# One of four sums in each feed-forward unit: VectorE's addition from PSUM, or a ScalarE copy and a GpSimd addition

## The chip, the cores and the metric

The kernel runs on one core of a Trainium2 chip. A core has a matrix engine (TensorE, PE in the profile; its weight loads are PEld), three engines that work on tiles (VectorE is DVE, ScalarE is ACT, GpSimd is POOL), an engine that issues transfers (SyncE, SP), and DMA queues. Each engine takes its instructions in a fixed order. Matrix products land in PSUM; all else lies in SBUF.

The metric is the device time of one execution in microseconds (us), as the median of several runs.

## The reference, cut to what matters

Two graph layers run one after the other on 128 graphs of 128 nodes with 256 features each, in fp32. Each layer ends with a feed-forward network over all nodes, with 1024 hidden units:

```python
# layer 0, after two graph-attention steps
h = layernorm(residual + h, g_ln1, b_ln1)
ff = relu(h @ w_ff1 + b_ff1) @ w_ff2 + b_ff2
x = layernorm(h + ff, g_ln2, b_ln2)
# layer 1, after 8-head attention with 4 relations
x = layernorm(src + attn_out, g1, beta1)
ff = gelu(x @ W1 + b1) @ W2 + b2
out = layernorm(x + ff, g2, beta2)
```

The change touches the first product of each of the two networks, `h @ w_ff1` and `x @ W1`.

## The kernel before, in words

**Tiling.** Four graphs make a group (512 nodes), so there are 32 groups. Five stages work on a group: load, graph attention (`gat`), the feed-forward of layer 0 with Relu (`ff0`), the attention of layer 1, and the feed-forward of layer 1 with Gelu (`ff1`). Every stage is a Python generator that yields a planned duration after each step. A loop at the end of the kernel keeps all stages of all groups in a heap by due time and always advances the earliest. So the stages of neighbouring groups are interleaved: while one group is in `ff1`, the next ones are in the attention and in `ff0`. Their steps repeat with a period of some 96 us.

**Order on the engines.** Between fixed planned times (`KEPT`, 280 to 3260 for TensorE) the order in which the loop emits TensorE's instructions is binding, and so is the order of SP's transfers. The other engines are ordered by the framework's scheduler, which works with its own estimates of time; no instruction of theirs is placed ahead of the TensorE instruction emitted before it. Every pool of buffers is shared by all stages. The PSUM pool `mm` has six buffers of one bank each: all products except `av` take one and give it back when the last reader is done.

**The feed-forward.** `feed_forward` (L289) computes the hidden layer with seven products in place of eight. The input and the weights are cut into halves in both directions; sums of the blocks are formed once (`weight_sums` for the weights, `moving_sums`, L283 to L286, on GpSimd for the moving side), and the seven block products are combined by additions. The hidden features are made in two units of two blocks each, `unit(0)` and `unit(2)`; I call them the first and the second unit. A unit has three PSUM tiles of 128x512, `chain`, `side` and `p`, and two SBUF tiles of twice that size, `lo` and `hi`, both named `fT`. The last index in `lo[:, :, 0]` picks one half of the nodes. A unit has four steps:

1. Products 1 into `chain` and 5 into `side`. ScalarE copies `chain` to half 0 of `lo` (L313) and `side` to half 1 of `hi` (L314).
2. Product 6 is added to `chain`, 2 goes to `p`, 3 is added to `side`. ScalarE copies `chain` to half 1 of `lo` (L320); VectorE adds `p` and `side` to the halves of `lo` (L321, L322).
3. Product 7 is added to `chain` (L307 records all of the products). VectorE adds `chain` to half 1 of `hi` (L325). ScalarE applies Relu or Gelu to `lo` (L327).
4. Product 4 is added to `chain`. ScalarE applies the function to `chain` into half 0 of `hi`, and to half 1 of `hi` in place (L333).

In the loop after `unit` the steps of the two units alternate: first, second, first, second, and so on. Each product is one instruction of 128x256 per block, which the trace shows as two matmuls, so a product of a unit is four matmuls. Between the steps of the units, other stages put their products. After step 4 comes the second product of the network (L350), which takes `lo` and `hi` as its weights.

**Other lines that the prediction names.** L239 scales rows in a layer norm on ScalarE, with factors that GpSimd computes (L233 to L237). L245 is the gain or offset of a norm on GpSimd, in pieces of 128x512 or 128x256. L351 adds the second product to the tokens on VectorE. L373 to L386 are the softmax of the graph attention: L373 and L384 on ScalarE, L380 and L381 on VectorE, L386 on GpSimd. L397 is the first product of the graph attention and L398 its copy by ScalarE; L405, L406 and L415 are its later products and copies. L429 and L435 are the query and key products of the attention, L449 the scores, L455 their maxima on VectorE, L459 the exponential on ScalarE, L461 its scaling on GpSimd, L475 the four masks of a graph (VectorE, 128x1024), L482 and L483 the values and their bias, L494 the weighted sum (`av`), L498 its copy by ScalarE, L532 and L533 the output product and its addition. L262 is a transposition on VectorE ahead of a pair of transfers. L260 is a copy after a transposition on TensorE, which only the first and the last groups use.

Of the kernel before, what the change touches and what calls it, by code (L numbers as in the profile page):

```python
# [57 lines left out]
def graph_layers(ctx: ExitStack, tc: tile.TileContext, a: dict, out: bass.AP):  # L58
# [8 lines left out]
    nc = tc.nc  # L67
# [156 lines left out]
    def normalised(y, first=0, n=G):  # L224

        y = y[:, first:first + n]
        mv = sm.tile([P, n, 2], F32, name="mv")
        for b in range(n):
            st = sm.tile([P, 6], F32, name="st")
            nc.vector.bn_stats(st, y[:, b])  # L230
            nc.vector.bn_aggr(mv[:, b], st)
        rstd = sm.tile([P, n], F32, name="rstd")
        nc.gpsimd.tensor_scalar(rstd, mv[:, :, 1], EPS, None, op0=OP.add)  # L233
        nmr = sm.tile([P, n], F32, name="nmr")
        nc.gpsimd.tensor_scalar(nmr, mv[:, :, 0], -1.0, None, op0=OP.mult)
        nc.gpsimd.tensor_tensor(rstd, rstd, mhalf[:, :n], OP.pow)
        nc.gpsimd.tensor_mul(nmr, nmr, rstd)  # L237
        for b in range(n):
            nc.scalar.activation(y[:, b], y[:, b], AF.Identity, bias=nmr[:, b:b + 1], scale=rstd[:, b:b + 1])  # L239

    def affine(y, k, b, n, engine=nc.gpsimd):


        for op, v in zip((OP.mult, OP.add), ln[k]):
            engine.tensor_tensor(y[:, b:b + n], y[:, b:b + n], v[:, None, :].to_broadcast([P, n, D]), op)  # L245
# [26 lines left out]
    def features(y, direct):  # L272

        t = t_tile().rearrange("p (b c n) -> p b c n", b=G, c=DC)
        blocks = t.rearrange("p b c n -> p (b c) n")
        transposed(y.rearrange("p b (c f) -> p (b c) f", f=P), blocks, direct, blocks)
        return t

    def moving_sums(hT):

        b11, b21, b12, b22 = (hT[:, h:h + G // 2, c] for h in (0, G // 2) for c in range(DC))
        t1, t2, t4 = (wk.tile([P, G // 2, N], F32, name=f"t{i}") for i in (1, 2, 4))
        nc.gpsimd.tensor_sub(t1, b12, b11)  # L283
        nc.gpsimd.tensor_sub(t2, b22, t1)
        nc.gpsimd.tensor_sub(b12, b22, b12)
        nc.gpsimd.tensor_sub(t4, t2, b21)  # L286
        return None, b11, b21, b22, t4, t1, t2, b12

    def feed_forward(y, before, direct, win, bin_, wout, func, by=G):  # L289


        hT = features(y, direct)
        yield TIMES["lead ff0" if before == "01" else "lead ff1"]
        hs = moving_sums(hT)
        yield TIMES["sums"]
        fT = [None] * FC

        def unit(f0):

            lo, hi = (wk.tile([P, 2, 2, T // 2], F32, name="fT", bufs=FC // 2) for _ in range(2))  # L300
            for i in range(2):
                fT[f0 + i] = lo[:, i].rearrange("p h t -> p (h t)")
                fT[FC // 2 + f0 + i] = hi[:, i].rearrange("p h t -> p (h t)")

            def product(p, k, first=False):
                for i in range(2):
                    nc.tensor.matmul(p[:, i], win[k][:, ts(f0 + i, P)], hs[k], start=first and i == 0, stop=True,  # L307
                                     skip_group_check=True)

            chain, side = (ps.tile([P, 2, T // 2], F32, name="mm") for _ in range(2))  # L310
            product(chain, 1, True)
            product(side, 5, True)
            nc.scalar.copy(lo[:, :, 0], chain)  # L313
            nc.scalar.copy(hi[:, :, 1], side)  # L314
            yield
            p = ps.tile([P, 2, T // 2], F32, name="mm")
            product(chain, 6)
            product(p, 2, True)
            product(side, 3)
            nc.scalar.copy(lo[:, :, 1], chain)  # L320
            nc.vector.tensor_add(lo[:, :, 0], lo[:, :, 0], p)  # L321
            nc.vector.tensor_add(lo[:, :, 1], lo[:, :, 1], side)  # L322
            yield
            product(chain, 7)
            nc.vector.tensor_add(hi[:, :, 1], hi[:, :, 1], chain)  # L325
            for i in range(2):
                nc.scalar.activation(lo[:, i], lo[:, i], func, bias=bin_[:, f0 + i:f0 + i + 1])  # L327
            yield
            product(chain, 4)
            for h, p in enumerate((chain, hi[:, :, 1])):  # L330
                for i in range(2):
                    f = FC // 2 + f0 + i
                    nc.scalar.activation(hi[:, i, h], p[:, i], func, bias=bin_[:, f:f + 1])  # L333
            yield

        units = [unit(0), unit(2)]
        for n, now in enumerate(((0,), (1,), (0,), (1,), (0,), (1,), (0,), (1,))):
            for u in now:
                next(units[u])
            if n in (2, 4):  # L340
                affine(y, before, n - 2, 2)
            yield TIMES["ff unit"]
        yield TIMES["ff2"]

        late = sorted(range(FC), key=lambda f: f % (FC // 2) // 2)
        for b2_ in range(0, G, 2):
            p = ps.tile([P, 2, D], F32, name="mm")
            for b in (b2_, b2_ + 1):
                for n, f in enumerate(late):
                    nc.tensor.matmul(p[:, b - b2_], fT[f][:, ts(b, N)], wout[:, f], start=n == 0, stop=n == FC - 1)  # L350
            nc.vector.tensor_add(y[:, b2_:b2_ + 2], y[:, b2_:b2_ + 2], p)  # L351
            yield TIMES["ff half"]
            if (b2_ + 2) % by == 0:
                normalised(y, b2_ + 2 - by, by)
        return y
# [313 lines left out]
```

## Time and profile before

| What | Value |
|---|---|
| median of 3 runs | 3207.63 us (3207.33 to 3208.44) |
| the profiled execution's own time | 3206.17 us |
| its span, first to last instruction | 3204.4 us |
| mean granted TensorE clock | 0.99 |
| busy: ScalarE | 1688.0 us |
| L325, the addition in question | 128 of 128x512, 81.5 us in all, 672 ns each |
| L320, a ScalarE copy of the same shape | 128, 586 ns each |
| L245 on GpSimd, 128x512 and 128x256 | 1276 ns and 739 ns each |

The profile is one execution. A row of a timeline gives the start and the duration in us, the engine, the line, the operation, the tiles (written <- read), the shapes and how many were merged into the row; in brackets follows how long the engine was idle before it and which instruction ended that. A row of waits gives who waited for whom, then the total in us, the number of times, and the longest. A wait for several things is put down to the one that came last by the profile, which can be the wrong one. The ends of matmuls are modelled, so a row of TensorE overlaps the next by some 0.2 us; the start of the next is the better mark.

### The profile page before, as it was taken

What the parts mean: (1) busy time and instruction counts of PE and PEld (TensorE: products, weight loads), DVE (VectorE), ACT (ScalarE), POOL (GpSimd) and SP (SyncE); (2) the same over time, 40 slices, a digit from 0 to 9 for tenths busy, and PEclk for the clock granted to TensorE, in tenths of its full rate; (3) what the DMA queues carried; (4) which work ended last, traced back from release to release, by engine and by line L of the source; (5) the groups of instructions that cost most, each with busy time, mean ns of one, the idle gap of its engine ahead of it and who ended that gap; (6) DMA issues with size and microseconds to landing.
All of it is one profiled execution on the core that took longest, in us unless ns stands there. A gap on an engine that the chain in (4) does not pass through costs nothing. (4 is left out here: it accounts for less than half of the span.)

```text
span 3204.4 us, 55197 instructions
## 1 busy us (share of the span) xinstructions
PE 3123.5 (97%) x20160; PEld 2381.1 (74%) x20160; DVE 2021.8 (63%) x3666; ACT 1688.0 (53%) x5063; POOL 1378.1 (43%) x1738
## 2 busy tenths in 40 slices
PE   7989999999999999999999999999999999999988
PEld 6756777777777777777777777777777777777666
DVE  3666666656566666576666576666576666576563
ACT  4435556555555455555455555455555465555443
POOL 2314345445345344345344345344345344345342
PEclk8999999999999999999999999999999999999999
DMA  4244454444454444454444454444454444453310
GB/s 163 60 106 97 105 116 106 103 101 97 104 118 104 104 99 100 101 121 103 106 99 100 100 122 102 107 98 101 100 122 100 108 94 102 103 122 82 83 34 14
DMA packets 1156399, 320.82 MB, mean 100 GB/s; under 512 B 902944, under 2 KB 1126688, under 8 KB 1156000
## 3 DMA queue, kind: packets, MB, share of 16 engines
q1 hardware_dynamic: 1156128, 317.29, 43.5%
q8 instruction: 160, 2.62, 0.3%
q14 instruction: 111, 0.91, 0.1%
HBM read 187.58 MB, written 129.62 MB: 99 GB/s over the span
## 5 line engine op out<-in xcount | busy, mean ns | idle before, releaser
L475 DVE SCALAR_TENSOR_TENSOR m<-adj,eT 128x1024 f32<-128x1024 f32 x512 | 598.5, 1212 | 240.7 <-DMA eT<-zd 178.2
L245 POOL TENSOR_TENSOR tok<-tok,ln_rows 128x512 f32<-128x512 f32 (+1 forms) x636 | 668.8, 1060 | 42.2 <-PE mm L256 14.8
L461 POOL TENSOR_TENSOR e<-e,s 128x512 f32<-128x512 f32 x256 | 266.4, 1041 | 661.0 <-DVE s L460 629.1
L459 ACT ACTIVATE e<-mm,nm 128x128 f32<-128x128 f32 x1024 | 360.0, 375 | 203.6 <-DVE nm L455 180.5
L482 PE MATMUL mm<-wv,T 128*128 128x512 f32 x1024 | 466.0, 598 | 0.0
L350 PE MATMUL mm<-wf,fT 128*128 128x256 f32 x2048 | 456.9, 381 | 0.0
L350 PE MATMUL mm<-w,fT 128*128 128x256 f32 x2048 | 455.6, 381 | 1.2 <-DVE v L483 1.2
L350 PEld LDWEIGHTS mm<-w,fT 128*128 128x128 f32 x2048 | 387.5, 190 | 74.7 <-issue 23.7
L350 PEld LDWEIGHTS mm<-wf,fT 128*128 128x128 f32 x2048 | 387.4, 190 | 62.3 <-ACT wh L406 7.9
L482 PEld LDWEIGHTS mm<-wv,T 128*128 128x128 f32 x1024 | 192.6, 191 | 200.2 <-issue 191.6
L239 ACT ACTIVATE tok<-tok,nmr,rstd 128x256 f32<-128x256 f32 x512 | 269.3, 594 | 136.4 <-POOL nmr L237 123.8
L351 DVE TENSOR_TENSOR tok<-tok,mm 128x512 f32<-128x512 f32 x128 | 87.8, 686 | 294.9 <-PE mm L350 283.0
L386 POOL TENSOR_TENSOR e<-e,s 128x512 f32<-128x512 f32 (+1 forms) x68 | 67.2, 989 | 470.4 <-DVE s L385 375.2
L494 PE MATMUL av<-m,v 128*32 128x128 f32 x8192 | 254.9, 276 | 6.0 <-DVE m L475 3.5
L494 PEld LDWEIGHTS av<-m,v 128*32 128x32 f32 x8192 | 218.2, 111 | 52.7 <-issue 43.5
L283 POOL TENSOR_TENSOR t<-T 128x256 f32<-128x256 f32 x64 | 46.6, 728 | 485.2 <-DMA T<-zd 485.2
L459 ACT ACTIVATION_READ_ACCUMULATOR e<-mm,nm 128x1 f32 x1024 | 219.4, 214 | 0.0
L455 DVE TENSOR_REDUCE nm<-mm 128x4 f32<-128x512 f32 x256 | 162.8, 676 | 60.3 <-PE mm L449 60.1
L483 DVE TENSOR_TENSOR v<-mm,bv 128x512 f32<-128x512 f32 x256 | 167.4, 683 | 49.3 <-PE mm L482 49.3
L307 PE MATMUL mm<-T,w 128*128 128x256 f32 x768 | 196.9, 386 | 0.2 <-ACT T L260 0.2
L307 PE MATMUL mm<-T,wf 128*128 128x256 f32 x768 | 193.6, 382 | 0.0
L373 ACT ACTIVATE e<-e,wh 128x128 f32<-128x128 f32 x240 | 77.7, 410 | 208.8 <-DMA e<-zsd 208.8
(123 smaller groups left out, 5093.0 us busy)
## 6 DMA issues: line engine op xcount, KB each, us to landing
zd<-e SPq DMA_DIRECT2D x496, 128.0 KB, 3.1
eT<-zd SPq DMA_DIRECT2D x124, 512.0 KB, 4.1
zd<-T SPq DMA_DIRECT2D x364, 128.0 KB, 4.4
T<-zd SPq DMA_DIRECT2D x91, 512.0 KB, 4.1
xt<-in_xT_dram SPq DMA_DIRECT2D x32, 512.0 KB
at<-in_adjT_dram SPq DMA_DIRECT2D x64, 256.0 KB, 6.2
tok<-in_x_dram SPq DMA_DIRECT2D x32, 512.0 KB
out_dram<-tok SPq DMA_DIRECT2D x31, 512.0 KB, 7.5
```

The lines of the kernel that those rows point to most:

```text
L239: nc.scalar.activation(y[:, b], y[:, b], AF.Identity, bias=nmr[:, b:b + 1], scale=rstd[:, b:b + 1])
L245: engine.tensor_tensor(y[:, b:b + n], y[:, b:b + n], v[:, None, :].to_broadcast([P, n, D]), op)
L307: nc.tensor.matmul(p[:, i], win[k][:, ts(f0 + i, P)], hs[k], start=first and i == 0, stop=True, skip_group_check=True)
L350: nc.tensor.matmul(p[:, b - b2_], fT[f][:, ts(b, N)], wout[:, f], start=n == 0, stop=n == FC - 1)
L351: nc.vector.tensor_add(y[:, b2_:b2_ + 2], y[:, b2_:b2_ + 2], p)
L455: nc.vector.tensor_reduce(nm, p, AX.X, OP.max, negate=True)
L459: nc.scalar.activation(eh[:, q], p[:, q], AF.Exp, bias=nm[:, q:q + 1], accum_out=s[:, q:q + 1])
L461: nc.gpsimd.tensor_mul(eh, eh, per_row(s, N))
L475: nc.vector.scalar_tensor_tensor(m, ab, r, eT, op0=OP.is_equal, op1=OP.mult)
L482: nc.tensor.matmul(p, hT[:, b, f], wv[:, f, r:r + 2], start=f == 0, stop=f == DC - 1)
L483: nc.vector.tensor_add(v[:, r:r + 2].rearrange("p r d -> p (r d)"), p.rearrange("p r d -> p (r d)"), bv[:, r * D:(r + 2) * D])
L494: last = nc.tensor.matmul(po[ts(q, DH), c], v[:, r, c * P + q * DH:c * P + (q + 1) * DH], ms[r][:, q // 2 * HC + c * 2 + q % 2], start=r = ...
```

## The change

Half 1 of `hi` was the sum of products 5 (`side`, copied by ScalarE) and of `chain` after product 7 (added from PSUM by VectorE). After the change the copy of `side` goes to half 0 of `hi`, which nothing else uses until step 4. In step 3 ScalarE copies `chain` to half 1, and GpSimd adds half 0 to it. All else is as before, and the result is the same sum. The lines below the edit move down by one.

```diff
             product(chain, 1, True)
             product(side, 5, True)
             nc.scalar.copy(lo[:, :, 0], chain)
-            nc.scalar.copy(hi[:, :, 1], side)
+            nc.scalar.copy(hi[:, :, 0], side)
             yield
...
             product(chain, 7)
-            nc.vector.tensor_add(hi[:, :, 1], hi[:, :, 1], chain)
+            nc.scalar.copy(hi[:, :, 1], chain)
+            nc.gpsimd.tensor_add(hi[:, :, 1], hi[:, :, 1], hi[:, :, 0])
             for i in range(2):
                 nc.scalar.activation(lo[:, i], lo[:, i], func, bias=bin_[:, f0 + i:f0 + i + 1])
```

There are 32 groups, two networks and two units in each, so every line of the edit stands for 128 instructions.

## The prediction

> **What bounds the kernel now.** I read four views, in this order: the page, the waits of TensorE, and the timelines of TensorE and the others over one period of the steady state (1600 to 1697 us).
>
> The page first. TensorE is busy 97% of the span, VectorE 63%, GpSimd 43%. An edit that moves work among the three slower engines can only matter where TensorE waits for one of them.
>
> ```profile
> PE 3123.5 (97%) x20160; PEld 2381.1 (74%) x20160; DVE 2021.8 (63%) x3666; ACT 1688.0 (53%) x5063; POOL 1378.1 (43%) x1738
> DVE  3666666656566666576666576666576666576563
> POOL 2314345445345344345344345344345344345342
> ```
>
> The waits of TensorE (columns: who waited for whom, us in total, times, longest) show one that recurs, on the addition to be replaced:
>
> ```profile
> PE mm L307 <- DVE fT L325: 16.3, 27, 1.2
> PE mm L415 <- POOL e L386: 10.3, 2, 6.3
> PE mm L405 <- POOL e L386: 8.0, 2, 4.4
> ...
> PE mm L307 <- POOL tok L245: 1.9, 2, 1.0
> ```
>
> The two for L386 fall at 218 and 247 us, in the start-up. The last row is the first one under another name: at 1183.62 and 1280.24 us TensorE stops at the same L307, and in the timeline GpSimd's L245 had long begun while VectorE's L325 had just ended (1182.79 plus half of 1.28). So 16.3 + 1.9 = 18.2 us in 29 stops hang on L325, nearly all in the Relu stage (ff0). One period there:
>
> ```profile
> 1659.31 1.89 PE L307 MATMUL mm<-T,wf 128*128 128x256 f32 x8
> 1661.03 3.60 PE L482 MATMUL mm<-wv,T 128*128 128x512 f32 x8
> 1665.20 1.97 PE L307 MATMUL mm<-t,wf 128*128 128x256 f32 x8 [0.57 <-DVE fT L325]
> 1667.00 1.90 PE L405 MATMUL mm<-wh,e 128*128 128x258 f32 x8
> ...
> 1659.25 4.61 DVE L475 SCALAR_TENSOR_TENSOR m<-adj,eT 128x1024 f32<-128x1024 f32 x4
> 1663.78 0.68 DVE L322 TENSOR_TENSOR fT<-fT,mm 128x512 f32<-128x512 f32 x1
> 1664.37 1.28 DVE L325 TENSOR_TENSOR fT<-fT,mm 128x512 f32<-128x512 f32 x2
> ...
> 1658.44 1.33 ACT L327 ACTIVATE fT<-fT,col 128x512 f32<-128x512 f32 x2
> 1660.60 2.08 ACT L239 ACTIVATE tok<-tok,nmr,rstd 128x256 f32<-128x256 f32 x4 [0.82 <-POOL nmr L237]
> 1664.38 2.08 ACT L239 ACTIVATE tok<-tok,nmr,rstd 128x256 f32<-128x256 f32 x4 [1.70 <-POOL nmr L237]
> ```
>
> The reader is to see: product 7 of both units is issued at 1659.31 and done by 1661.03. Product 4 accumulates into the same PSUM tile, so it waits until the tile is read. The reader, VectorE's L325, stands behind four masks (L475, 4.61 us) and L322, and the first L325 ends at 1665.05. TensorE, done with L482 at 1664.63, stands idle for 0.57 us. ScalarE has gaps of 0.82 and 1.70 us just then. TensorE is busy 95.68 us of the 96.25 us from 1600.36 to 1696.61: this is the period's only idle time.
>
> **What the Trainium skill says.** "PSUM — Partial Sum Buffer", The four PSUM rules: GpSimd has no way into PSUM; hence the copy by ScalarE ahead of the addition. The trace agrees as far as it goes (no GpSimd row reads mm). "GPSIMD Engine Reference", 3.1 Elementwise: about 2.5 cycles an element as the floor with two inputs, at 1.2 GHz some 2.1 ns. The trace agrees: L245 takes 1276 ns for 512 elements and 739 for 256, so 2.10 ns each. "SBUF — State Buffer", Who interferes with whom: a VectorE instruction with two SBUF inputs excludes a GpSimd one that reads. The trace agrees: L380 (two SBUF inputs) took 1.19 us at 1650.62, beside an L245, and 0.69 us at 1683.43, beside nothing.
>
> **The change, part by part.** I read the order of instructions and the waits that the changed program is built with (no times are in them). TensorE's order differs only in the first 280 us, SP's not at all; both have 62 ScalarE table loads. Numbers of lines are those of before.
>
> *Line 314's other target* (half 0 for half 1): 128 copies as before, nothing.
>
> *Removed:* 128 VectorE additions of 672 ns, 86 us, and 18.2 us of TensorE waiting, if nothing else is late.
>
> *Added on ScalarE:* 128 copies like L320's (586 ns), 75 us. Relu stage: the first copy stands behind the two L327 and needs its product 7 (four of the eight matmuls, so half of 1.72 us: 1660.17; ScalarE reacts about 0.2 us after a start, as L314 does at 1651.74 to 1651.54): 1660.37 to 1660.96. Then four L239 to about 1662.95, then the second copy, to 1663.45. TensorE wants the first at 1664.63 and the second at 1665.49: 3.6 and 2.0 us early. The stop goes, whole.
>
> *Added on GpSimd:* 128 additions. No row is a plain 128x512 sum of two full tiles; the nearest are L461 (1041 ns, one input broadcast along the row) and L245 (1276). I take 1.28 us: 164 us, GpSimd at 48%. It reads both inputs, so the two ends are 1.04 and, if VectorE excludes it once for a whole instruction such as L380, 1.28 + 0.69 = 1.97 us. Queued behind the first addition in the Relu stage are two L245 (0.74, 1.28) and L237, on which the second block of L239 waits: L236 ends at 1662.24, addition to 1663.5, L245 to 1665.5, L237 to 1665.7, against 1664.34 before.
>
> *Added waits on ScalarE:* L333 for half 1 waits for the addition; L333 for half 0 too, since it overwrites the addition's second input. Behind them stand the copies L406 and L498. Carried on with the same durations: addition 1663.5, L333 to 1664.45, L327 to 1665.8, L239 to 1667.85, L333 on the first chain to 1668.65, three L406 to 1669.45, four L333 to 1671.1, L406 and L498 to 1671.75 (before: 1672.05). TensorE, 0.57 us earlier, wants its PSUM tiles for L449 at 1670.15 (the first chain and the first L406, free by 1669.0) and for L350 at 1671.25 (the second L406, 1669.2). At least 1.1 us is left. The second addition ends at 1668.2 and GpSimd has nothing due before 1674.5.
>
> The Gelu stage (ff1) has no stop now, and must not get one:
>
> ```profile
> 1615.23 2.56 ACT L327 ACTIVATE fT<-fT,col 128x512 f32<-128x512 f32 x4
> 1617.70 0.35 ACT L498 COPY oT<-av 128x256 f32<-128x256 f32 x1
> 1617.95 1.70 ACT L333 ACTIVATE fT<-fT,col 128x256 f32<-128x256 f32 x4
> ...
> 1618.82 1.03 PE L307 MATMUL mm<-t,w 128*128 128x256 f32 x4
> ```
>
> There the copies stand behind four L327 and L498, where L333 began: 1617.95 to 1618.55, and to 1619.0. Product 4 starts at 1618.82 and 1620.55; ScalarE's L260 released an L307 within 0.05 us at 3163.74. That leaves 0.2 us, and in three other periods (1039, 2195, 2580 us) product 4 follows the start of L498 by the same 1.12 us. The additions run 1618.6 to 1621.2, L333 ends at 1623.6 in place of 1622.46; the PSUM tile due first is wanted at 1624.9 and free at 1622.8. Two L245 start up to 5 us late, to end at 1622.7; VectorE's L533 needs them at 1630.42. Cost nothing; without that slack, the excess once a period.
>
> *Start-up and end.* In group 0 the first chain's L333 now stands behind L373, which waits for a transfer until 77.06 us; L350 runs out of other work at about 76.9 and gets its half at 78.8: 1.9 us. In group 1 the addition stands behind eight L245 that end at 110.28, so L333 comes 1.4 us late. TensorE's later stops for L386 (4.4 and 6.3 us) may absorb some of it. I take 2.3 us of 0 to 5. In the last group the additions wait for L245 until 3178.92 and just meet L350: 0, at worst 1.
>
> *Sum:* -18.2 + 2.3 = -15.9 us. Against the profiled execution's own 3206.17 us (span 3204.4 and 1.8 around it): 3190.3. The median, 3207.63, lies 1.46 above that execution: 3191.7, so 3192.
>
> **Rivals.**
> (A) The wait only changes its name. ScalarE's queue is full from 1658 to 1672 in the Relu stage; if L237, and with it the first L239 block, comes 2.6 us later than 1660.56, the second copy is as late as L325 was. For it: TensorE's weight loads waited 0.20 us on L333 and 0.33 us on L406 here. Against it: the 1.1 us above. Then 3207.6 + 2.3 = 3210.
> (B) Slower, by one mechanism: GpSimd holds ScalarE in the Gelu stage. ScalarE waits for both additions before it frees the chains; if exclusion by VectorE makes each last 2.6 us, they end at 1623.8, L333 frees the first chain at 1625.6, and L429's second tile, wanted at 1624.9, is 0.7 us late in 30 periods: 3192 + 21 + more of the same in the start-up, some 3215. It decides from 2.5 us an addition, where the loss passes the 0.57 us gained. For it: L380's doubled time. Against it: VectorE's work in those windows (L483, L475, L262) has one SBUF input.
> That the change doesn't do what it says is closed by the built order: 128 additions gone, 128 copies and 128 sums there.
>
> **How the numbers follow.** Forecast 0.80, its own range 3187 to 3200 (start-up 0 to 5, the Gelu slack failing by up to 0.1 us in 29 periods, a part of the stop staying). A 0.11, B 0.09. The range reaches 3203 to take in a part of A, where half of the stop stays: 3186 to 3203. About 0.2% (6.4 us) is what a measurement can tell from no change. Faster by more: 0.80; within: 0.11; slower: 0.09.
>
> **What would show it.** Right: the row of TensorE's waits for L325 gone; GpSimd's additions near 1.28 us, VectorE near 1936 us busy, ScalarE near 1763; a period of 95.7 us. Wrong: TensorE idle before product 4 for ScalarE's copy (my 0.2 us in the Gelu stage), before L449 or L350 for L333 or L406, or start-up stops that grow by over 5 us.

## The result and the profile after

The changed kernel took 3191.89 us (median of 4 runs, 3191.65 to 3194.92), the kernel before beside it 3207.48: a ratio of 0.9953, 95% interval 0.9936 to 0.997. The forecast was 3192.0. Run twice more it came out at 3198.0 and 3197.3, ratios of 0.9969 [0.9958, 0.9981] and 0.9974 [0.9963, 0.9985] against the kernel before of the same series. So the gain is 9 to 16 us. All three medians lie in the range of the prediction, but the sum behind it held only because two errors cancelled, which is luck, and that is what most of the experiments are about.

In the changed kernel every line from L326 on is one higher than in the prediction, and L325 and L326 are ScalarE's copy and GpSimd's addition. Its profiled execution took 3191.92 us with a span of 3190.1. The busy line of its page, and below it three rows of TensorE's waits:

```profile
PE 3122.4 (98%) x20160; PEld 2379.2 (75%) x20160; DVE 1945.5 (61%) x3538; ACT 1745.1 (55%) x5191; POOL 1535.8 (48%) x1866
```

```profile
PE av L495 <- DVE v L484: 3.2, 3, 2.3
...
PE mm L533 <- DVE v L484: 1.2, 2, 0.9
...
PE mm L351 <- ACT fT L334: 0.6, 1, 0.6
```

The row that led the table before (L325, 16.3 us) is gone, and no row took its place with more than a few stops. The listed waits fell from 70.4 to 56.1 us, by 14.3, and the span fell by 14.3 too. It looks as if the sum were clear: the stop gone, a little lost elsewhere. It is not so, as the next view shows. The Relu stage of the period that the prediction showed:

```profile
1656.64 1.89 PE L307 MATMUL mm<-T,wf 128*128 128x256 f32 x8
1657.70 0.58 ACT L325 COPY fT<-mm 128x512 f32<-128x512 f32 x1 [0.66 <-PE mm L307]
1658.36 3.60 PE L483 MATMUL mm<-wv,T 128*128 128x512 f32 x8
1659.42 1.28 POOL L326 TENSOR_TENSOR fT<-fT 128x512 f32<-128x512 f32 x1
1660.16 0.57 ACT L325 COPY fT<-mm 128x512 f32<-128x512 f32 x1
...
1661.80 1.89 PE L307 MATMUL mm<-t,wf 128*128 128x256 f32 x8
...
1663.52 1.90 PE L406 MATMUL mm<-wh,e 128*128 128x258 f32 x8
```

The reader is to see the copies well ahead of product 4 (1661.80), which carries no bracket now. And then to take differences of starts. From L483 to L406 there are 5.16 us; before, from 1661.03 (L482) to 1667.00 (L405), there were 5.97. The stop had cost 0.81 us, and the idle column had shown 0.57: it counts from a modelled end of L482, 3.60 us after its start, while an undisturbed product follows after 3.44; and the eight products took 1.80 instead of 1.72 us from start to start after the stop. Over the 28 Relu stages between 300 and 2950 us, with six in which the kernel before was later still (1.9 us in all), that makes 28 x 0.81 + 1.9 = 24.6 us.

The same comparison can follow the whole run: the start of each output projection (L533), less the start of the same one before (L532), in the two profiled executions. I call it the offset.

| Where (time before) | Offset of the changed kernel, us |
|---|---|
| 162 | +2.8 |
| 302 | +6.3 |
| 1620 | -2.7 |
| 2934 | -13.1 |
| 3120 | -14.9 |

So the start loses 6.3 us, not 2.3; the steady part gains 19.4, less than the 24.6 that the stops were worth; and the last groups gain 1.8 (in the two repetitions they lost 0.2 and gained 1.2). Two questions follow: what gives back several us of the steady gain, and what costs so much in the start?

### The profile page after: what moved, and what is told of

It is laid out like the page before. It is cut to its first block, busy times and chain, and to the rows that moved or that the text cites. A ratio compares the mean times of both kernels' runs of the same rounds, so it can differ in the third digit from the quotient of the medians.

```text
span 3190.1 us, 55111 instructions
## 1 busy us (share of the span) xinstructions
PE 3122.4 (98%) x20160; PEld 2379.2 (75%) x20160; DVE 1945.5 (61%) x3538; ACT 1745.1 (55%) x5191; POOL 1535.8 (48%) x1866
## 4 chain that ended last, share of the span: by engine, by line
PE 84%; DMA 5%; DVE 5%; ACT 2%; SPq 2%; POOL 1%; issue 1%; ACTq 0%; DVEq 0%; POOLq 0%
PE mm L351 25%; PE mm L307 21%; PE mm L483 11%; PE av L495 6%; PE mm L450 4%; PE mm L398 3%; PE mm L436 3%; PE mm L430 3%; PE mm L533 3%; DVE m L476 2%; DMA eT<-zd 2%; DMA zd<-e 2%; PE mm L416 2%; PE mm L406 2%; SPq L265 1%
## 5 line engine op out<-in xcount | busy, mean ns | idle before, releaser
L476 DVE SCALAR_TENSOR_TENSOR m<-adj,eT 128x1024 f32<-128x1024 f32 x512 | 598.7, 1213 | 199.1 <-DMA eT<-zd 189.5
L245 POOL TENSOR_TENSOR tok<-tok,ln_rows 128x512 f32<-128x512 f32 (+1 forms) x636 | 671.0, 1062 | 41.0 <-PE mm L256 15.3
L483 PE MATMUL mm<-wv,T 128*128 128x512 f32 x1024 | 465.8, 598 | 0.2 <-ACT e L460 0.2
L351 PE MATMUL mm<-wf,fT 128*128 128x256 f32 x2048 | 456.8, 381 | 0.6 <-ACT fT L334 0.6
L351 PE MATMUL mm<-w,fT 128*128 128x256 f32 x2048 | 455.5, 381 | 0.0
L351 PEld LDWEIGHTS mm<-w,fT 128*128 128x128 f32 x2048 | 387.1, 190 | 73.7 <-issue 23.5
L351 PEld LDWEIGHTS mm<-wf,fT 128*128 128x128 f32 x2048 | 386.9, 190 | 63.5 <-ACT fT L334 8.9
L483 PEld LDWEIGHTS mm<-wv,T 128*128 128x128 f32 x1024 | 192.3, 191 | 201.2 <-issue 194.7
L239 ACT ACTIVATE tok<-tok,nmr,rstd 128x256 f32<-128x256 f32 x512 | 268.8, 593 | 72.4 <-POOL nmr L237 72.4
L326 POOL TENSOR_TENSOR fT<-fT 128x512 f32<-128x512 f32 x128 | 161.6, 1273 | 146.0 <-ACT fT L325 146.0
L484 DVE TENSOR_TENSOR v<-mm,bv 128x512 f32<-128x512 f32 x256 | 169.8, 684 | 79.4 <-PE mm L483 79.4
```

Source lines behind the costliest of these rows:

```text
L326: nc.gpsimd.tensor_add(hi[:, :, 1], hi[:, :, 1], hi[:, :, 0])
L476: nc.vector.scalar_tensor_tensor(m, ab, r, eT, op0=OP.is_equal, op1=OP.mult)
L483: nc.tensor.matmul(p, hT[:, b, f], wv[:, f, r:r + 2], start=f == 0, stop=f == DC - 1)
L484: nc.vector.tensor_add(v[:, r:r + 2].rearrange("p r d -> p (r d)"), p.rearrange("p r d -> p (r d)"), bv[:, r * D:(r + 2) * D])
```

## Experiments

Each experiment states its own ratio to the kernel before of the same series; offsets and counts are from its profiled execution.

### Where the gain is made: one stage at a time

A flag in `feed_forward` chooses the form; it is `before == "01"` for Relu only, `before == "11"` for Gelu only.

```diff
-            nc.scalar.copy(hi[:, :, 0], side)
+            nc.scalar.copy(hi[:, :, 0 if split else 1], side)
...
-            nc.scalar.copy(hi[:, :, 1], chain)
-            nc.gpsimd.tensor_add(hi[:, :, 1], hi[:, :, 1], hi[:, :, 0])
+            if split:
+                nc.scalar.copy(hi[:, :, 1], chain)
+                nc.gpsimd.tensor_add(hi[:, :, 1], hi[:, :, 1], hi[:, :, 0])
+            else:
+                nc.vector.tensor_add(hi[:, :, 1], hi[:, :, 1], chain)
```

> The new form only in the first feed-forward layer (Relu), all groups. Theory: the whole steady gain of 0.82 us a period comes from the Relu stage, where product 4 waited for VectorE's addition; the Gelu stage had no such stop. So 3191 to 3193, as the changed kernel; TensorE has no wait at product 4. Rival: part of the gain came from the Gelu stage (VectorE's queue shortened there by 0.67 us for each unit lets later steps of TensorE go earlier): then between, about 3199.

Measured: 3192.85 us, 0.9955 [0.9943, 0.9968].

> The new form only in the second layer (Gelu). Theory: no steady gain, the wait of product 4 in the Relu stage stays at about 0.6 us in each period in TensorE's table of waits: 3207 us, as the kernel before, within 2. Rival (part of the gain comes from the Gelu stage): about 3199.

Measured: 3206.89 us, 1.0 [0.9992, 1.0009], with the stop in place (TensorE's waits of this kernel; its L330 is VectorE's addition):

```profile
PE mm L308 <- DVE fT L330: 17.1, 28, 1.2
```

The theory holds: the whole gain comes from the Relu stage, and the Gelu half of the change by itself is worth nothing. The Relu-only profile also had 11 stops at the output projection behind L488 (L484 of the changed kernel), 5.4 us, that the kernel before does not have.

### Who reads the tile, and who adds

VectorE in place of GpSimd for the sum of the two halves:

```diff
-            nc.gpsimd.tensor_add(hi[:, :, 1], hi[:, :, 1], hi[:, :, 0])
+            nc.vector.tensor_add(hi[:, :, 1], hi[:, :, 1], hi[:, :, 0])
```

> The copies as in the changed kernel, but the sum of the two halves, now both in SBUF, is made by VectorE and not by GpSimd. Theory: what TensorE waited for is that the PSUM tile is read, not that the sum is made; the ScalarE copy frees the tile, and the addition may come late. So as the changed kernel, 3191 to 3194 us, the steady gain of 0.82 us a period whole; a stop could come only through ScalarE, whose Relu of the tile waits for VectorE's addition behind the masks. Rival: the gain needs VectorE's 0.67 us per unit taken off its queue: then most of the gain goes, about 3205.

Measured: 3224.17 us, 1.0054 [1.0041, 1.0066]: slower than both, which neither theory expected. The timeline of this kernel in its Relu stage, where L326 is VectorE's addition:

```profile
1673.37 4.64 POOL L245 TENSOR_TENSOR tok<-tok,ln_rows 128x512 f32<-128x512 f32 x3
1673.51 1.68 DVE L326 TENSOR_TENSOR fT<-fT 128x512 f32<-128x512 f32 x1
1673.61 1.89 PE L307 MATMUL mm<-t,wf 128*128 128x256 f32 x8
...
1675.71 1.17 DVE L326 TENSOR_TENSOR fT<-fT 128x512 f32<-128x512 f32 x1
1676.81 0.68 DVE L484 TENSOR_TENSOR v<-mm,bv 128x512 f32<-128x512 f32 x1
1677.54 0.70 PE L406 MATMUL mm<-wh,e 128*128 128x258 f32 x2 [0.73 <-DVE v L484]
```

Product 4 (1673.61) comes 3.44 us after the start of L483, without a stop: for it the reader alone matters, as the theory has it. But the next wait ends on VectorE: the second L484, which frees the PSUM tile for L406, stands behind two additions of 1.68 and 1.17 us. L406 stopped 26 times, 19.0 us. The additions are long because both inputs lie in SBUF and GpSimd's L245 runs beside them: of the 128, the 66 beside no GpSimd work took 0.69 us on average, and the 60 wholly beside it 1.34. This is what the Trainium skill says in "SBUF — State Buffer", Who interferes with whom: VectorE's second port is GpSimd's, and one of the two has it at a time. The addition of the kernel before, with one input in PSUM, took 0.68 us in either case. So taking the sum off VectorE was as needed as the copy.

### What GpSimd's additions cost

Without them (one term of the sum is left out):

```diff
-            nc.gpsimd.tensor_add(hi[:, :, 1], hi[:, :, 1], hi[:, :, 0])
```

> The changed kernel without the addition: the two halves are copied by ScalarE and not summed (one term of the feed-forward sum is left out). It shows what GpSimd's 128 additions cost in all. Theory: nothing in the steady periods; in the start, where a Relu is waited for, at most the 3.3 us that the prediction put there: 3188 to 3192. Rival: GpSimd's additions hold ScalarE in a way that costs TensorE in every period: 3170 to 3180.

Measured: 3185.49 us, 0.993 [0.9917, 0.9944], 12.5 us below the changed kernel in the same series (3198.0). That is below the theory's 3188 and above the rival's 3180. My theory fell: the additions do cost something in the steady periods. The offset of this kernel fell by 24.9 us between 302 and 2934, in even steps, and it had no stop at the output projection behind the bias addition (L483 here, L484 of the changed kernel). Two places in the changed kernel give the difference away.

*The output projection.* The chain that leads to its stop, in the changed kernel:

```profile
1109.71 0.38 SPq L267 DMA_DIRECT2D eT<-zd  x1
...
1114.35 3.70 PE L483 MATMUL mm<-wv,T 128*128 128x512 f32 x8
1115.03 2.36 DVE L476 SCALAR_TENSOR_TENSOR m<-adj,eT 128x1024 f32<-128x1024 f32 x2 [1.07 <-DMA eT<-zd]
...
1120.71 1.10 PE L533 MATMUL mm<-wo,oT 128*128 128x256 f32 x4 [0.94 <-DVE v L484]
```

The masks (L476) wait for the transfer of `eT`, the transposed weights of the attention; behind them on VectorE stands L484, whose PSUM tile L533 needs. The transfer is late because SP issues in order: it stands behind others whose chain goes back to the Relu stage. SP's rows in the period of the table below, changed kernel:

```profile
1188.44 3.35 SPq L265 DMA_DIRECT2D zd<-T  x4
...
1200.01 0.34 SPq L371 DMA_DIRECT2D e<-zsd  x1
1200.39 3.24 SPq L265 DMA_DIRECT2D zd<-e  x4
...
1206.18 0.38 SPq L267 DMA_DIRECT2D eT<-zd  x1
```

VectorE had finished the transposition that `zd<-e` carries at 1197.91; the transfer left only behind `e<-zsd`, the row of scores of the graph attention. One period, each time relative to the start of the value product named (L482 before, L483 after, L488 in the kernel of the next section, which puts the addition behind `nmr`):

| Event | before | after | addition behind `nmr` |
|---|---|---|---|
| GpSimd makes `nmr` (L237), from the value product of the Relu stage | +3.07 | +4.24 | +2.97 |
| ScalarE's second block of L239 | +3.34 | +4.97 | +3.20 |
| SP issues the row of scores `zsd` (L368), from the next value product | -3.31 | -1.54 | -2.84 |
| SP issues `eT`, from the value product after that | -6.93 | -5.13 | -6.47 |
| masks start, from the same | -0.92 | -0.44 | -0.92 |

GpSimd's addition stands ahead of the product that makes `nmr`. That delays the norm, the transposition and its transfers by 1.2 to 1.8 us (of the 1.6 at L239, 1.2 come from `nmr`; the rest is ScalarE's own queue, in which L334 and L328 stand ahead), and SP carries the delay some 25 us on to `eT`. In the kernel before the row of these masks carries no wait; now the transfer of `eT` is what they wait for last, and in a period with slower transfers, as at 1115 (5.3 us from the issue of `eT` to the masks, against 4.7 in the period of the table), they start at +0.68 and L533 stops.

*The Gelu stage.* The later masks delay the norm there as well. In the timeline of the changed kernel, a period with the loss and one without:

```profile
1226.83 2.08 ACT L239 ACTIVATE tok<-tok,nmr,rstd 128x256 f32<-128x256 f32 x4 [1.64 <-POOL nmr L237]
1229.94 3.60 PE L483 MATMUL mm<-wv,T 128*128 128x512 f32 x8
1232.93 1.06 ACT L325 COPY fT<-mm 128x512 f32<-128x512 f32 x2
1233.66 1.10 PE L307 MATMUL mm<-t,w 128*128 128x256 f32 x4
```

```profile
1322.20 2.08 ACT L239 ACTIVATE tok<-tok,nmr,rstd 128x256 f32<-128x256 f32 x4 [1.24 <-POOL nmr L237]
1325.71 3.60 PE L483 MATMUL mm<-wv,T 128*128 128x512 f32 x8
1328.30 1.07 ACT L325 COPY fT<-mm 128x512 f32<-128x512 f32 x2
1329.14 1.03 PE L307 MATMUL mm<-t,w 128*128 128x256 f32 x4
```

L239 starts 3.11 us ahead of L483 in the first and 3.51 in the second. ScalarE's copy stands behind it (and behind the table load, four L328 and L499), so product 4 starts 3.72 us after L483 instead of 3.43. No bracket marks this stop. Measured from L483 to the projection after product 4, the stretch is 4.30 us when undisturbed and up to 4.67 otherwise. It follows the start of the masks, counted as in the table: in the 27 periods between 302 and 2934 us of the changed kernel it was 4.30 wherever they started at -0.91 or earlier, 4.37 at -0.80, 4.54 at -0.64, and 4.65 to 4.67 from -0.52 on. It was longer by over 0.1 us in 11 of these 27 periods (3.9 us with the small ones), in 16 of 27 in each of its two repetitions (5.2 and 5.0 us), and in none of the kernel before, of Relu only, of Gelu only, or of the kernel without the addition.

### The addition moved behind `nmr`

The addition is emitted in step 4, and for the first unit in the Relu stage the scheduler is told to put it behind the latest `nmr` product:

```diff
-            nc.gpsimd.tensor_add(hi[:, :, 1], hi[:, :, 1], hi[:, :, 0])
             for i in range(2):
...
             product(chain, 4)
+            total = nc.gpsimd.tensor_add(hi[:, :, 1], hi[:, :, 1], hi[:, :, 0])
+            if f0 == 0 and before == "01" and nmrs:
+                tc.add_manual_dep(total.ins, nmrs[-1].ins.name, mybir.DependencyInfo(
+                    mybir.DependencyClass.NoSync, mybir.DependencyReason.DATA), reason="behind nmr")
```

> The changed kernel with the first unit's addition in the Relu stage put behind the product that makes nmr on GpSimd, so that ScalarE normalises first and applies Relu afterwards. Theory: the addition ahead of that product made the transposed features, and with them SyncE's later transfers down to the attention's masks, 1.4 to 1.7 us late, which left the output projection's PSUM tile without slack; without it the stops before the projection are gone and the time comes near the kernel without the addition: 3186 to 3190, some 4 below the changed kernel. Rival: the stops are the transfers' own variation: as the changed kernel.

> The changed kernel a third time, for comparison with the next three on one chip: 3191 to 3198, with two to five stops before the output projection, by 1 to 2.5 us in all, and about 6 us behind before's times at 300 us.

Measured in one series: 3189.19 us, 0.9948 [0.9935, 0.996], against 3197.3 for the changed kernel, 0.9974 [0.9963, 0.9985], whose profile had four stops at the projection (2.1 us). In the timeline of the moved one (its L239 is `nmr`, L332 the addition, L241 the norm):

```profile
1179.38 0.20 POOL L239 TENSOR_TENSOR nmr<-nmr,rstd 128x4 f32<-128x4 f32 x1
...
1179.53 1.27 POOL L332 TENSOR_TENSOR fT<-fT 128x512 f32<-128x512 f32 x1
1179.61 2.08 ACT L241 ACTIVATE tok<-tok,nmr,rstd 128x256 f32<-128x256 f32 x4 [0.84 <-POOL nmr L239]
```

Nothing of the addition was saved, only its place changed, and ScalarE now normalises ahead of the Relus. The stops at the projection are gone, the Gelu stretch is 4.30 us in all 27 periods, and the offset falls by 25.5 us between 302 and 2934 instead of 19.4. So the place of one 1.27 us instruction in GpSimd's queue, with the order of ScalarE that comes with it, and not its load, was what gave back 6 us in the first profile of the changed kernel and 9 in the others (16.2 gained in each).

### The loss in the start

With the form of before in groups 0, 1 and 31 (`split = 2 <= g < NG - 1`):

> The new form only in groups 2 to 30; groups 0, 1 and 31 keep VectorE's addition. Theory: the changed kernel gains 0.82 us in each steady period and loses about 6 us in the first 300 us, because the two early groups, in which a Relu's inputs are waited for at once, and the order of TensorE's instructions there are disturbed by the change. Then this kernel keeps the gain and drops the loss: 3186 us, 6 below the changed kernel. Rival: the loss of the start is not made by the change (the granted clock in the first 60 us and other variation between executions), or any edit in the middle shifts the order of the start as well: then 3191 to 3193, as the changed kernel.

Measured: 3192.4 us, 0.9956 [0.9943, 0.9968]. Its offset at 302 us was -0.9, so the loss of the start was gone; but it fell by only 14.9 us from there to 2934, with six stops at the projection (2.9 us) and Gelu stretches longer by over 0.1 us in 18 of 27 periods. So the time is the rival's, 3191 to 3193, and not the theory's 3186, though for another reason than the rival's. TensorE was also granted more clock in this execution (0.83 against 0.74 from 40 to 60 us, 1.00 against 0.91 from 80 to 120, in the kernel before and the changed one), so part of the -0.9 may be the clock's.

With the new form in groups 0 and 1 alone (`split = g < 2`):

> The new form only in groups 0 and 1. Theory: it loses 4 to 7 us in the first 300 us and gains 0.8 in one Relu stage: 3211 to 3214. Rival (the loss of the start is variation between executions): 3205 to 3209.

Measured: 3217.72 us, 1.0037 [1.0024, 1.005], 11.7 us slower. Its offset was +9.9 at 302 us, and then +9.9 to +7.9 to the end. The loss is the change's own, and here larger than expected: in this order TensorE stopped once for 9.9 us behind VectorE's L488 (L484 of the changed kernel), where the kernel before stopped for 6.3 us behind the softmax.

> The changed kernel once more. Theory: 3190 to 3195, the gain of 0.83 us in each steady period again at one place (product 4 of the Relu stage). Of the about 6 us that it was behind before's times at 300 us, the part made by TensorE's clock in the first 120 us changes from execution to execution, the part made by waits (0.6 for a Relu, 2.4 for masks and values, 1.2 for a PSUM tile) comes back at the same places. Rival: the 6 us were variation altogether, and the offset at 300 us is within 2 us of zero.

Measured: 3198.02 us, 0.9969 [0.9958, 0.9981], above the 3190 to 3195 expected. Offset +7.4 at 302 us, with TensorE's clock as in the first profile of the changed kernel and stops at the same places (0.6 us at L351, 1.4 at L430, 0.8 at L436). The loss repeats; in the third series it was +6.8.

### Both mends together

Relu stage only, groups 2 to 30 only, addition behind `nmr`; VectorE adds from PSUM elsewhere. The edit is the two flags joined (`before == "01" and 2 <= g < NG - 1`) with the move above.

> As the run before, but with the new form only in the Relu stage of groups 2 to 30; VectorE adds from PSUM everywhere else. Theory: the steady gain whole (0.83 us in 28 periods), no stops before the output projection, and no loss in the start: 3182 to 3186. Rival: the loss in the start is not the change's own and stays or comes and goes: 3186 to 3190.

Measured: 3183.36 us, 0.9928 [0.9916, 0.9941], 22.6 us below the kernel before and 13.9 below the changed kernel of the same series. The offset is +2.1 at 302 us and falls by 25.5 to 2934. It is faster than both. Its clock in the start was that of the kernel before (0.74 and 0.91 in the two stretches named above), so +2.1, and not -0.9, is the fairer mark: by it the changed form costs some 4 to 5 us in the start.

### From what length GpSimd decides

Further additions behind each one, on a half tile that the Relu or Gelu overwrites:

```diff
             nc.gpsimd.tensor_add(hi[:, :, 1], hi[:, :, 1], hi[:, :, 0])
+            nc.gpsimd.tensor_add(hi[:, :, 0], hi[:, :, 0], hi[:, :, 0])
```

> The changed kernel with one more GpSimd addition of the same size behind each one, on a half tile that a Relu or Gelu overwrites later, so that its input comes after about 2.5 us instead of 1.27. Rival B of the prediction put the point from which GpSimd decides at 2.5 us an addition: by it about 3211. From the changed kernel's trace the first chain would come free at 1622.4 to 1622.6 in the Gelu stage, the projection's second tile is wanted at 1622.3: 0.1 to 0.3 us late in 30 periods, 3195 to 3201. If the hold doesn't matter to TensorE, 3192.

Measured: 3200.24 us, 0.9977 [0.9967, 0.9987]. That lies in the expected 3195 to 3201, but in the same series the changed kernel had 3198.0 us, 0.9969 [0.9958, 0.9981]: no difference is shown. The added instruction took 1.04 us, not 1.27, so each input came after 2.31 us, short of rival B's 2.5.

> Two more GpSimd additions behind each one, about 3.8 us in all. By rival B's mechanism each further 1.27 us per addition delays the pair's end by 2.5 us, and all of it falls on the projection's tile: 2.6 to 3.2 us in 30 periods over the changed kernel, 3270 to 3290. If other buffers take part of it up: 3210 to 3250. If the hold doesn't matter: 3192.

Measured: 3286.52 us, 1.0245 [1.0231, 1.0259]; each input came after 1.27 + 2 x 1.04 = 3.35 us. The size is as rival B's mechanism has it, the place is not, so the size is no support for it. TensorE's waits of this kernel (L353 is the network's second product, L336 the Relu or Gelu of `hi`):

```profile
PE mm L353 <- ACT fT L336: 52.7, 58, 3.1
PE mm L353 <- DVE tok L536: 14.7, 18, 2.3
```

In all 28 steady periods the first of these falls on the second product of the Relu stage (1.27 and 0.48 us), not on the query product's tile in the Gelu stage. So a hold by GpSimd begins to decide somewhere between 2.31 and 3.35 us, at another place.

## Why the prediction was right, and where its steps were not

**The bound and the cause: right.** TensorE waited because the reader of its PSUM tile stood behind masks, and all of the gain is in the Relu stage.

**The copies in the Relu stage: right.** The first was to start 1.06 us after product 7 and the second to end 4.14 us after it; they did so after 1.06 and 4.09 us. The additions took 1.27 us (1.28 taken).

**The stop: mis-sized.** 18.2 us was the sum of an idle column; from start to start the stops were worth 24.6 us. The prediction's own table had both starts in it, and what stands ahead of it says that they are the better mark. The period was to be 95.7 us; without a stop it is 95.4.

**"L237 to 1665.7, against 1664.34 before": right, and not followed on.** Counted from the value product it was 1.1 us later in this period and 1.2 in that of the table (1.4 expected). The slack that I then checked, "at least 1.1 us", was that of the Relu stage, and it was there: TensorE did not stop at L450 or at the steady L351. But L237 has another consumer: the norm, a transposition, and then SP's queue. I had read that SP's order is unchanged and did not ask whether its first entry comes later. This is the step that failed. It brought the stops at the projection (1.2 to 2.2 us a run) and, through the later norm, those of the Gelu stage.

**"Cost nothing; without that slack, the excess once a period": the slack of 0.2 us failed** in about half of the periods by up to 0.37 us, 4 to 5 us in all. The cause was not the copy by itself (Gelu only costs nothing), but the delay that came from the Relu stage.

**The start: mis-sized,** 6.3 to 7.4 us where I took 2.3 of 0 to 5. The Relu that I had named came: L351 stopped at 78.85 us, but that put TensorE back by 0.8 us, not 1.9. The larger part came later, where nothing was costed: 2.5 us between 148 and 176 us (the first masks late by 1.20, TensorE's order changed) and 1.5 by 200 us (a PSUM tile behind VectorE's L484). Without GpSimd's additions 4.4 us of offset were still there at 302, so most of it doesn't come from them; I take the changed order of TensorE and VectorE for its cause, which no run shows by itself. How much of the first 1.2 us, there by 70 us, is the change's own and how much varies from run to run, I didn't separate.

**The sum.** For the profiled execution: a steady gain of 25.5 us, as the moved addition reaches it (24.6 from the stops; 0.9 not assigned), less 3.9 (Gelu stage), 1.2 (projection) and 1.0 not found, 19.4 in all; +6.3 in the start; -1.8 after 2934: -14.9 at the last projection, -14.3 in the span. Forecast were -18.2 + 2.3 = -15.9. The stop was taken 7 us too small, the losses 8 us too small; that the two nearly cancelled was luck.

**The signs.** The row for L325 is gone and the additions took 1.27 us. VectorE was busy 1945.5 us (1936 expected) and ScalarE 1745.1 (1763); I did not follow that up. Two of the signs of being wrong came as well: TensorE late before product 4 for ScalarE's copy in the Gelu stage, and a start that lost over 5 us.

**The rivals.** A's own mechanism, a second copy in the Relu stage as late as L325 was, did not come. That a late L237 moves the wait elsewhere did, in the Gelu stage and at the projection, and it took back a quarter to a good third of the steady gain. B's wait on the query product's tile did not come even with additions of 3.35 us; the hold that did stop TensorE, at the second product of the Relu stage, begins a good us above the 1.27 us of one addition.

## What to carry to other kernels

Take the price of a recurring stop from the starts of the instructions around it, in a period with and one without, not from the idle column. When an instruction is put into a queue, follow each one behind it to its last consumer, through transfers and the issuing queue, even if the next stage shows slack: the delay may land a quarter of a period later. A short addition can be free or cost several us by its place alone, so after an edit look at which chain it now stands in front of, and move it, before judging the edit.

## What the runs showed that I had not expected

- A VectorE addition with both inputs in SBUF took 0.69 us alone and 1.34 us on average beside GpSimd; the one with an input in PSUM stayed at 0.68.
- A GpSimd addition of a tile to itself took 1.04 us for 128x512, one of two tiles 1.27 us.
- Stops of up to 0.37 us of TensorE carried no mark in the timeline and filled no row of the waits; eleven of them made 3.9 us.
- The medians of one kernel in three series were 3191.9, 3198.0 and 3197.3 us, those of the kernel before beside it 3207.5, 3207.5 and 3206.0. In the changed kernel the masks wait for a transfer and so vary from period to period; the Gelu stage and the projection account for some 2 of the 6 us between its series, and the rest is not explained.
